# The last certain expert tile in two halves, and the two results of a token side by side: loaded in eight pieces, added by two engines, stored on two queues

## The chip, the cores and the metric

The kernel runs on one core of one Trainium2 chip. The time is device microseconds of that core for one execution. The kernel before took 618.88 us, the median of 6 runs (617.77 to 619.91). Lower is better. Engines are called as in the profile: PE (TensorE matmul) and PEld (its weight loads), DVE (VectorE), ACT (ScalarE), POOL (GpSimd) and SP (SyncE, which here only issues transfers).

## The reference, cut to what matters

The input is x of 4 batches with 512 tokens of 128 features, 2048 tokens in all. Attention comes first and its result is added to x. Then every token goes to two of eight experts, and the two weighted results are added to x:

```
combine = sum(one_hot(top2 experts) * weight)          # two experts per token
hact = up * gelu(gate)                                 # 512 hidden features per expert
out  = sum over the token's two experts of weight * (hact @ down_w[expert].T)
return x + out
```

## The kernel before, in words

**Attention** fills the first part of the execution. A planner (`route`, `plan`) works out, batch by batch, the two experts of each token and scatters each token's normalized row, with its weights and with the numbers of the rows where its two results belong, into an array `slots` in DRAM, so that tiles of 128 slots belong to one expert each. There are 39 possible tiles (`TILES`), of which 35 are certain (`sure`); the last four stand in nested `tc.If` blocks and run only where the counts call for them. In the profiled execution none of the four ran: the groups of L753, L754 and L766 have 35 instructions each.

**One expert tile t** has four steps. `load` (L683) issues three transfers on SP's queue: the rows, the gate and up weights, the down weights. `prepare` (L722) transposes the rows (PE L727, ACT L729) and takes each row's weight and target row (DVE L731, L736, L738). `up` (L742) does the 16 recorded matmuls of gate and up into one PSUM tile (PE L748), then Gelu over 128x512 (ACT L753) and the product of Gelu and up (DVE L754, 128x512, tile `act`). `down` (L756) does the 8 recorded matmuls with the down weights (PE L761), scales by the token's weight (DVE L766, tile `ye`), and scatters the 128 rows to the array `parts` in DRAM by an indirect transfer from POOL (L770), followed by a small POOL memset (L220).

**The order is written out by hand** (`tc.manual_schedule`). In the loop of L789 tile t's `up` comes first, then `prepare(t+1)`, then `down(t-1)`. So at the last certain tile, 34, DVE's queue holds: the product of tile 34, then the scaling of tile 33; after the loop `down(34)` follows. Then every engine passes the branches of the four spare tiles (L801). Where they are skipped, POOL runs one instruction (`INC_SWDGE_SEM`, at L801) that raises the semaphores which the skipped scatters would have raised.

**The end** (L808 to L817): a token's two results stand in `parts` at row p\*8 + k\*4 + c of their batch, for partition p, column c of 4 and choice k of 2. So the first results of a partition's four tokens lie together, and the second results behind them. SP waits for all scatters, then issues four loads of 512 KB, one per batch (L811). DVE adds, per batch, the first results and then the second results to x, 128x512 each (L814, eight instructions). ACT's queue stores each batch, 256 KB, when its two adds are done (L817). After that each engine comes to the end of the program (L863): a DRAIN, and a barrier in which POOL and SP wait for all.

```
for b in range(B):
    follow(nc.sync.dma_start(yy[:, b], both[b]), added)
for b in range(B):
    for k in range(TOP_K):
        nc.vector.tensor_tensor(xs[b], xs[b], yy[:, b, k * NT : (k + 1) * NT], ALU.add)
    nc.scalar.dma_start(out[b].rearrange("(p c) d -> p c d", p=P), xs[b])
```

Of the kernel before, what the change touches and what calls it, by code (L numbers as in the profile page):

```python
# [9 lines left out]
F32 = mybir.dt.float32  # L10
# [3 lines left out]
ALU = mybir.AluOpType  # L14
# [9 lines left out]
TOP_K = 2  # L24
# [7 lines left out]
def tile_attention_then_moe(  # L32
# [100 lines left out]
    def numbers(what, shape, pattern, base=0, channel=0):  # L133
        t = const.tile(shape, F32, tag=what, name=what)
        nc.gpsimd.iota(
            t, pattern, base=base, channel_multiplier=channel, allow_small_or_imprecise_dtypes=True
        )
        return t

    token = numbers("token", [P, B, NT], [[TOP_K * S, B], [1, NT]], base=-NONE, channel=TOP_K * NT)  # L140
    first = numbers("first", [P, E], [[N, E]])
    expert = numbers("expert", [P, E], [[1, E]])
    tile_no = numbers("tile_no", [P, TILES], [[1, TILES]])
# [78 lines left out]
    def follow(ins, scatters):  # L222

        for scatter in scatters:
            tc.add_manual_dep(
                ins.ins, scatter.ins.name,
                mybir.DependencyInfo(mybir.DependencyClass.Sync, mybir.DependencyReason.DATA),
                reason="reads what was scattered",
            )
# [267 lines left out]
    def route(g, hn, hT):  # L497
# [54 lines left out]
        for k in range(TOP_K):  # L552
# [2 lines left out]
        row = t8("row")  # L555
        nc.vector.tensor_tensor(row, top, wide(token[:, g, :]), ALU.mult)
        nc.vector.scalar_tensor_tensor(
            hn[:, :, D + E :], hits[:, 1], float(NT), row, ALU.mult, ALU.add
        )
        if late:  # L560
            yield from pause(1)
# [107 lines left out]
    def experts():  # L669


        NCH = WIDE // P
        GF = S // WIDE

        def value(at, most):
            return nc.values_load(
                at, engines=[mybir.EngineType.SP], min_val=0, max_val=most,
                skip_runtime_bounds_check_because="plan() bounds it: a tile is of an expert or spare",
            )

        got = {}

        def load(t):  # L683
            while t not in plans:
                assert others
                advance(others)
            new = {}
            if t >= sure:
                if not count:
                    count.append(nc.values_load(  # L690
                        needed[B - 1],
                        engines=[
                            mybir.EngineType.SP, mybir.EngineType.PE, mybir.EngineType.DVE,
                            mybir.EngineType.Activation, mybir.EngineType.Pool,
                        ],
                        min_val=0, max_val=TILES,
                        skip_runtime_bounds_check_because="plan() bounds it: it counts tiles",
                    ))
                new["cond"] = count[0] > t - STARTS[-2]
            mine, e_at, slot_at, scatters = plans[t]  # L700
            e = value(e_at, E - 1)
            at = value(slot_at, spare)
            gu = p4.tile([P, F2], F32, tag="gu", name=f"gu_{t}")
            dn = p4.tile([P, NF, D], F32, tag="down", name=f"down_{t}")
            xt = p4.tile([P, NCH, ROW], F32, tag="xt", name=f"xt_{t}")

            rows = nc.sync.dma_start(
                xt, slots[bass.ds(at, WIDE), :].rearrange("(c p) d -> p c d", p=P), **new
            )
            follow(rows, scatters)  # L710
            for scatter in filled[len(scatters) :]:
                tc.declare_no_dep(rows.ins, scatter.ins, reason="to slots that no tile has yet")
            read.append(rows)
            nc.sync.dma_start(
                gu, gu_t[:, bass.ds(e, 1), :].rearrange("p o f -> p (o f)"), **new
            )
            nc.sync.dma_start(
                dn, down_t[:, bass.ds(e, 1)].rearrange("p o f d -> p (o f) d"), **new
            )
            got[t] = xt, gu, dn  # L720

        def prepare(t):  # L722

            xt, gu, dn = got[t]
            tp = ps_tp.tile([P, NCH, P], F32, tag="tp", name=f"tp_e_{t}")
            for c in range(NCH):
                nc.tensor.transpose(tp[:, c, :], xt[:, c, 0:D], ident)  # L727
            xT = p2.tile([P, NCH * P], F32, tag="xeT", name=f"xeT_{t}")
            nc.scalar.copy(xT, tp.rearrange("p c t -> p (c t)"))  # L729
            of = small.tile([P, NCH, 2, E], F32, tag="of", name=f"of_{t}")  # L730
            nc.vector.tensor_tensor(  # L731
                of, xt[:, :, D:].rearrange("p c (i e) -> p c i e", i=2),
                plans[t][0].unsqueeze(1).to_broadcast([P, NCH, 2, E]), ALU.mult,
            )
            w = small.tile([P, NCH, 2], F32, tag="w", name=f"w_{t}")
            nc.vector.tensor_reduce(w, of, AX.X, ALU.add)  # L736
            row = small.tile([P, NCH], U32, tag="row", name=f"row_{t}")
            nc.vector.tensor_scalar_add(row, w[:, :, 1], float(NONE))  # L738
            act = p2.tile([P, NF, WIDE], F32, tag="act", name=f"act_{t}")
            got[t] = xT, gu, dn, w, row, act  # L740

        def up(t, f0):  # L742
            xT, gu, act = got[t][0], got[t][1], got[t][5]
            ps = ps_sc.tile([P, 2, GF, WIDE], F32, tag="sc", name=f"gu_{t}_{f0}")
            for g in range(GF):
                for j in range(2):
                    at = j * F + (f0 + g) * P
                    nc.tensor.matmul(  # L748
                        ps[:, j, g, :], gu[:, at : at + P], xT, start=True, stop=True
                    )  # L750
            yield
            ge = p3.tile([P, GF, WIDE], F32, tag="ge", name=f"ge_{t}_{f0}")
            nc.scalar.activation(ge, ps[:, 0], AF.Gelu)  # L753
            nc.vector.tensor_tensor(act[:, f0 : f0 + GF, :], ge, ps[:, 1], ALU.mult)  # L754

        def down(t):  # L756
            _, _, dn, w, row, act = got.pop(t)
            ps = ps_tp.tile([P, NCH, D], F32, tag="tp", name=f"dn_{t}")
            for c in range(NCH):
                for f in range(NF):  # L760
                    nc.tensor.matmul(  # L761
                        ps[:, c, :], act[:, f, c * P : (c + 1) * P], dn[:, f, :],
                        start=(f == 0), stop=(f == NF - 1),
                    )
            y = p3.tile([P, NCH, D], F32, tag="ye", name=f"ye_{t}")
            nc.vector.tensor_tensor(  # L766
                y, ps, w[:, :, 0:1].to_broadcast([P, NCH, D]), ALU.mult
            )
            for c in range(NCH):
                apart(added, nc.gpsimd.indirect_dma_start(  # L770
                    parts, bass.IndirectOffsetOnAxis(ap=row[:, c : c + 1], axis=0),
                    y[:, c, :], None, bounds_check=TOP_K * N - 1, oob_is_err=False,
                ))

        def ahead(t):

            for u in (t + 1, t + 2):
                if u < TILES and u not in loaded and (u in plans or u == t + 1):
                    load(u)
                    loaded.add(u)  # L780

        loaded, count = set(), []
        sure = TILES - SPARE_TILES
        ahead(-1)
        yield
        ahead(0)
        prepare(0)
        yield
        for t in range(sure):  # L789
            yield from up(t, 0)  # L790
            yield
            if t + 1 < sure:
                if t + 1 not in loaded:
                    ahead(t)
                prepare(t + 1)
            if t > 0:
                down(t - 1)
                ahead(t)
                yield
        down(sure - 1)  # L800
        with ExitStack() as inner:  # L801
            for t in range(sure, TILES):
                inner.enter_context(tc.If(count[0] > t - STARTS[-2]))
                prepare(t)
                yield from up(t, 0)
                ahead(t)
                down(t)
        both = parts.rearrange("(b p r) d -> b p r d", b=B, p=P)  # L808
        yy = p2.tile([P, B, TOP_K * NT, D], F32, tag="exT", name="yy")
        for b in range(B):  # L810
            follow(nc.sync.dma_start(yy[:, b], both[b]), added)  # L811
        for b in range(B):
            for k in range(TOP_K):
                nc.vector.tensor_tensor(  # L814
                    xs[b], xs[b], yy[:, b, k * NT : (k + 1) * NT], ALU.add
                )
            nc.scalar.dma_start(out[b].rearrange("(p c) d -> p c d", p=P), xs[b])  # L817

    hs, qkv, plans, needed, others = {}, {}, {}, {}, []
    filled, added = [], []  # L820
# [46 lines left out]
```

## Time and profile before

| what | value |
|---|---|
| median of 6 runs | 618.88 us (617.77 to 619.91) |
| the profiled execution's own time | 618.49 us |
| its span, first to last instruction | 616.78 us (1.71 us lie around it) |
| PE busy | 562.4 us (91% of the span) |
| DVE, ACT, POOL busy | 388.9, 352.0, 332.1 us |
| the last PE matmul ends | 599.84 us |
| loads of `parts` (L811) | 4, 512 KB each, first issued at 603.89 us |
| adds (L814) | 8, 690 ns each on average |
| stores (L817) | 4, 256 KB each, last issued at 613.43 us |

The page's PE row is at 9 or more tenths through nearly all of the span; the last slices, of 15.4 us each, fall to 8 and 0. Only those last 20 us hold instructions that the change touches. Times in what follows are microseconds from the start of the span. The granted TensorE clock was 0.977 on average.

### The profile page before, as it was taken

To read this page: it belongs to the slowest core of one execution; us is meant where nothing else is said; L and a number is where in the kernel's file an instruction comes from. 1 tells how busy PE (TensorE), PEld (TensorE's weight loads), DVE (VectorE), ACT (ScalarE), POOL (GpSimd) and SP (SyncE) were. 2 spreads that over 40 slices of the span, in tenths; PEclk is the share of its full clock that TensorE was granted. 3 is DMA by queue.
4 is the path that set the end of the run, shared out by engine and by line. 5 is a ranking of instruction groups with operands and counts; after the bars stand their busy time and mean duration, and the time that the engine had idled before them with its cause. 6 is when DMAs were issued, how large, how long until landed. Compare 5 with 4: busy or idle time off the path is not lost.

```text
span 616.8 us, 10390 instructions
## 1 busy us (share of the span) xinstructions
PE 562.4 (91%) x3363; PEld 344.8 (56%) x3363; DVE 388.9 (63%) x973; ACT 352.0 (57%) x896; POOL 332.1 (54%) x338
## 2 busy tenths in 40 slices
PE   3779999999999999999999999999989999499980
PEld 1235445446654544566454455654446898499980
DVE  1568666566677688666777875577893278144443
ACT  2467767776678766767776677677764122022220
POOL 3356554555557458755764686457575145433340
PEclk9899999999999999999999999999999999699995
DMA  8990000000000000200000005000002378589945
GB/s 237 300 236 1 2 0 2 1 0 2 2 1 0 1 2 20 69 8 2 0 1 0 12 25 173 2 2 1 1 16 82 104 257 253 192 258 311 321 163 205
DMA packets 38231, 50.32 MB, mean 82 GB/s; under 512 B 4115, under 2 KB 26517, under 8 KB 38176
## 3 DMA queue, kind: packets, MB, share of 16 engines
q1 hardware_dynamic: 34592, 43.50, 23.0%
q0 software_dynamic: 2144, 4.46, 2.0%
q10 hardware_dynamic: 1440, 1.67, 0.8%
q8 instruction: 28, 0.46, 0.3%
q14 instruction: 27, 0.22, 0.1%
HBM read 36.25 MB, written 15.29 MB: 84 GB/s over the span
## 4 chain that ended last, share of the span: by engine, by line
PE 69%; issue 8%; DVE 7%; POOL 6%; ACT 5%; DMA 5%; POOLq 0%; SPq 0%; DVEq 0%
PE sc L272 18%; PE av L315 18%; PE tp L305 16%; PE qp L254 5%; PE yp L339 5%; POOL parts L770 3%; DMA parts<-ye,row 3%; ACT ex L287 2%; PE gu L748 2%; DVE nmax L279 1%; ACT exT L415 1%; POOL slots L585 1%; ACT qT L256 1%; DMA yy<-parts 1%; DVE exT L417 1%
## 5 line engine op out<-in xcount | busy, mean ns | idle before, releaser
L296 POOL TENSOR_SCALAR ex<-ex,rden 128x512 f32<-128x512 f32 x128 | 221.1, 1729 | 168.1 <-DVE rden L295 166.3
L287 ACT ACTIVATE ex<-sc,nmax 128x512 f32<-128x512 f32 x256 | 176.1, 706 | 0.6 <-DVE nmax L279 0.6
L279 DVE TENSOR_REDUCE nmax<-sc 128x2 f32<-128x1024 f32 x128 | 150.5, 1217 | 8.0 <-PE sc L272 7.7
L305 PE MATMUL tp<-ident,ex 128*128 128x128 f32 x1024 | 131.3, 276 | 7.0 <-ACT exT L415 3.4
L272 PE MATMUL sc<-kT,qT 64*128 64x512 f32 x512 | 129.6, 623 | 8.2 <-ACT ex L287 7.5
L305 PEld LDWEIGHTS tp<-ident,ex 128*128 128x128 f32 x1024 | 112.9, 141 | 42.2 <-issue 24.6
L315 PE MATMUL av<-exT,v 128*64 128x512 f32 x512 | 128.4, 605 | 0.6 <-DVE exT L417 0.6
L415 ACT COPY exT<-tp 128x512 f32<-128x512 f32 x128 | 75.5, 590 | 49.0 <-PE tp L305 49.0
L272 PEld LDWEIGHTS sc<-kT,qT 64*128 64x128 f32 x512 | 43.9, 186 | 91.7 <-issue 52.0
L748 PE MATMUL gu<-xeT,gu 128*128 128x128 f32 x560 | 73.1, 285 | 10.9 <-ACT xeT L729 9.3
L770 POOL DMA_INDIRECT parts<-ye,row x35 | 34.4, 984 | 77.0 <-DVE ye L766 52.9
L295 DVE RECIPROCAL rden<-den 128x2 f32<-128x2 f32 x128 | 21.1, 165 | 86.5 <-ACT ex L287 82.7
L748 PEld LDWEIGHTS gu<-xeT,gu 128*128 128x128 f32 x560 | 67.0, 196 | 12.5 <-ACT xeT L729 9.7
L297 DVE TENSOR_SCALAR ex<-ex,rden 128x512 f32<-128x512 f32 x128 | 65.4, 511 | 4.5
L753 ACT ACTIVATE ge<-gu 128x512 f32<-128x512 f32 x35 | 20.9, 598 | 81.2 <-PE gu L748 63.3
L417 DVE COPY exT<-tp 128x512 f32<-128x512 f32 x64 | 44.0, 688 | 29.9 <-PE tp L305 29.8
L315 PEld LDWEIGHTS av<-exT,v 128*64 128x64 f32 x512 | 32.9, 136 | 51.1 <-issue 46.9
L754 DVE TENSOR_TENSOR act<-ge,gu 128x512 f32<-128x512 f32 x35 | 24.0, 686 | 58.2 <-ACT ge L753 31.5
L287 ACT ACTIVATION_READ_ACCUMULATOR ex<-sc,nmax 128x1 f32 x256 | 56.7, 221 | 0.0
L256 ACT ACTIVATE qT<-qp 128x512 f32<-128x512 f32 x32 | 19.1, 597 | 65.0 <-PE qp L254 65.0
L425 ACT COPY exT<-tp 128x512 f32<-128x512 f32 x64 | 39.6, 618 | 0.3 <-PE tp L305 0.3
L761 PE MATMUL dn<-down,act 128*128 128x128 f32 x280 | 38.3, 281 | 0.7 <-DVE act L754 0.5
(136 smaller groups left out, 435.3 us busy)
## 6 DMA issues: line engine op xcount, KB each, us to landing
gu<-in_gate_up_t_dram SPq DMA_DIRECT2D x37, 512.0 KB
down<-in_down_t_dram SPq DMA_DIRECT2D x37, 256.0 KB
slots<-blank SPq DMA_DIRECT2D x13, 720.0 KB
xt<-slots SPq DMA_DIRECT2D x37, 72.0 KB
yy<-parts SPq DMA_DIRECT2D x4, 512.0 KB
x<-in_x_dram SPq DMA_DIRECT2D x4, 256.0 KB
out_dram<-x ACTq DMA_DIRECT2D x4, 256.0 KB
parts<-ye,row POOLq DMA_INDIRECT x35
```

What stands on the lines that cost most here:

```text
L272: nc.tensor.matmul(sc[:, j, :], qT[p][half, t * P : (t + 1) * P], kT[half, :], start=True, stop=True)
L279: nc.vector.tensor_reduce(nmax, sc, AX.X, ALU.max, negate=True)
L287: nc.scalar.activation(ex[:, j, :], sc[:, j, :], AF.Exp, bias=nmax[:, j : j + 1], accum_out=den[:, j : j + 1],)
L296: nc.gpsimd.tensor_scalar_mul(ex[:, 0, :], ex[:, 0, :], rden[:, 0:1])
L297: nc.vector.tensor_scalar_mul(ex[:, 1, :], ex[:, 1, :], rden[:, 1:2])
L305: nc.tensor.transpose(tp[:, c, :], ex[:, j, c * P : (c + 1) * P], ident)
L315: nc.tensor.matmul(av[j * DH : (j + 1) * DH, :], v[:, c, :], exT[:, j, c, :], start=(c == 0), stop=(c == NT - 1),)
L415: nc.scalar.copy(*copies[0])
L417: nc.vector.tensor_copy(*copies[1])
L425: nc.scalar.copy(*copies[1])
L748: nc.tensor.matmul(ps[:, j, g, :], gu[:, at : at + P], xT, start=True, stop=True)
L770: apart(added, nc.gpsimd.indirect_dma_start(parts, bass.IndirectOffsetOnAxis(ap=row[:, c : c + 1], axis=0), y[:, c, :], None, bounds_check ...
```

## The change

Four things are changed together, all in the last 22 us; the program before them issues the same instructions in the same order.

1. **Halves.** The last certain tile's `up` is done as two halves of 256 columns: 8 recorded matmuls into one PSUM tile, 8 into another, two Gelus of 128x256 and two products of 128x256. `down` is split into `product` (matmuls) and `results` (scaling and scatter). On DVE the order is now: first half's product, scaling of tile 33, second half's product, scaling of tile 34.
2. **Rows side by side.** A token's two results go to rows p\*8 + c\*2 + k.
3. **Eight loads and split adds.** A piece is half the columns of a batch: 256 KB of results, 2 KB per partition in one run. SP issues eight loads. The adds are 128x256, two per piece: pieces 1, 3 and 5 on POOL, pieces 0, 2, 4, 6 and 7 on DVE.
4. **Eight stores** of 128 KB, 1 KB per partition: pieces 0, 2, 4, 6 on ACT's queue, pieces 1, 3, 5, 7 on SP's queue, behind the loads.

In the instruction order of the changed kernel each first add waits for the semaphore of its own load and each second add for the first. The eighth load uses the semaphore of the second load and waits until that one has landed. SP's store of piece 5 uses the semaphore of the store of piece 0 and waits for it too.

```diff
-    token = numbers("token", [P, B, NT], [[TOP_K * S, B], [1, NT]], base=-NONE, channel=TOP_K * NT)
+    token = numbers("token", [P, B, NT], [[TOP_K * S, B], [TOP_K, NT]], base=-NONE, channel=TOP_K * NT)
...
-            hn[:, :, D + E :], hits[:, 1], float(NT), row, ALU.mult, ALU.add
+            hn[:, :, D + E :], hits[:, 1], 1.0, row, ALU.mult, ALU.add
...
-        def up(t, f0):
+        def up(t, f0, n=GF):
...
-            ps = ps_sc.tile([P, 2, GF, WIDE], F32, tag="sc", name=f"gu_{t}_{f0}")
-            for g in range(GF):
+            ps = ps_sc.tile([P, 2, n, WIDE], F32, tag="sc", name=f"gu_{t}_{f0}")
+            for g in range(n):
...
-        for t in range(sure):
+        for t in range(sure - 1):
             yield from up(t, 0)
             yield
-            if t + 1 < sure:
-                if t + 1 not in loaded:
-                    ahead(t)
-                prepare(t + 1)
+            if t + 1 not in loaded:
+                ahead(t)
+            prepare(t + 1)
             if t > 0:
                 down(t - 1)
                 ahead(t)
                 yield
+
+        halves = [up(sure - 1, f0, GF // 2) for f0 in range(0, NF, GF // 2)]
+        for half in halves:
+            next(half)
+        rows = product(sure - 2)
+        for half in halves[:-1]:
+            next(half, None)
+        results(sure - 2, rows)
+        next(halves[-1], None)
+        ahead(sure - 1)
         down(sure - 1)
...
-        both = parts.rearrange("(b p r) d -> b p r d", b=B, p=P)
-        yy = p2.tile([P, B, TOP_K * NT, D], F32, tag="exT", name="yy")
-        for b in range(B):
-            follow(nc.sync.dma_start(yy[:, b], both[b]), added)
-        for b in range(B):
+
+        both = parts.rearrange("(b p c k) d -> b p c (k d)", b=B, p=P, k=TOP_K)
+        yy = p2.tile([P, B, NT, TOP_K, D], F32, tag="exT", name="yy")
+        half = NT // 2
+        pieces = [(b, slice(c, c + half)) for b in range(B) for c in range(0, NT, half)]
+        for b, c in pieces:
+            follow(
+                nc.sync.dma_start(yy[:, b, c].rearrange("p c k d -> p c (k d)"), both[b, :, c]),
+                added,
+            )
+        for i, (b, c) in enumerate(pieces):
+            by = nc.gpsimd if i in (1, 3, 5) else nc.vector
             for k in range(TOP_K):
-                nc.vector.tensor_tensor(
-                    xs[b], xs[b], yy[:, b, k * NT : (k + 1) * NT], ALU.add
-                )
-            nc.scalar.dma_start(out[b].rearrange("(p c) d -> p c d", p=P), xs[b])
+                by.tensor_tensor(xs[b][:, c], xs[b][:, c], yy[:, b, c, k], ALU.add)
+        for i, (b, c) in enumerate(pieces):
+            (nc.sync if i % 2 else nc.scalar).dma_start(
+                out[b].rearrange("(p c) d -> p c d", p=P)[:, c], xs[b][:, c]
+            )
```

More of the change, by code (lines that the diff above doesn't have):

```diff
@@ L751, in up, with product @@
             yield
-            ge = p3.tile([P, GF, WIDE], F32, tag="ge", name=f"ge_{t}_{f0}")
+            ge = p3.tile([P, n, WIDE], F32, tag="ge", name=f"ge_{t}_{f0}")
             nc.scalar.activation(ge, ps[:, 0], AF.Gelu)
-            nc.vector.tensor_tensor(act[:, f0 : f0 + GF, :], ge, ps[:, 1], ALU.mult)
-        def down(t):
-            _, _, dn, w, row, act = got.pop(t)
+            nc.vector.tensor_tensor(act[:, f0 : f0 + n, :], ge, ps[:, 1], ALU.mult)
+        def product(t):
+            dn, act = got[t][2], got[t][5]
             ps = ps_tp.tile([P, NCH, D], F32, tag="tp", name=f"dn_{t}")
@@ L764, in down, with results @@
                     )
+            return ps
+        def down(t):
+            results(t, product(t))
+        def results(t, ps):
+            _, _, _, w, row, _ = got.pop(t)
             y = p3.tile([P, NCH, D], F32, tag="ye", name=f"ye_{t}")
```

## The prediction

> **What bounds the kernel now.** I read the page's chain first, then the chain of waits from 585 us on, then the timeline of the last 20 us, then the lines L801 and L863. PE sets the pace up to about 600 us; the change touches only what follows. The chain there:
>
> ```profile
> 585.27 18.29 DMA parts<-ye,row
> 603.56 0.02 issue
> ...
> 603.89 0.34 SPq L811
> ...
> 604.75 5.87 DMA yy<-parts
> ...
> 610.65 0.70 DVE x L814
> ...
> 612.71 0.69 DVE x L814
> ```
>
> Columns are start, length, what. SP is released at 603.56, loads from 603.89, DVE starts the third batch at 610.65 when its load has landed, and the last add ends at 613.40. The last store is issued at 613.43; SP passes its wait for it at 615.46, and 1.32 us of waits and barrier end the span at 616.78. The 18.29 us belong to POOL's queue: its last scatter starts at 600.44 and ends at 601.41, and SP's release comes with the end of POOL's INC_SWDGE_SEM (602.09 to 603.62).
>
> How that last scatter came about, from the timeline (start, length, engine, line, operation):
>
> ```profile
> 597.30 0.60 ACT L753 ACTIVATE ge<-gu 128x512 f32<-128x512 f32 x1 [2.14 <-PE gu L748]
> ...
> 597.93 0.69 DVE L754 TENSOR_TENSOR act<-ge,gu 128x512 f32<-128x512 f32 x1 [1.53 <-ACTq L801]
> 598.54 0.28 DVE L766 TENSOR_TENSOR ye<-dn,w 128x128 f32<-128x128 f32 x1
> ...
> 598.68 1.16 PE L761 MATMUL dn<-down,act 128*128 128x128 f32 x8 [0.52 <-DVE act L754]
> ...
> 599.87 0.29 DVE L766 TENSOR_TENSOR ye<-dn,w 128x128 f32<-128x128 f32 x1 [1.05 <-PE dn L761]
> ```
>
> PE waits 0.52 us for the product of tile 34, then the chain Gelu, product, matmul, scaling runs with nothing beside it.
>
> **Halves: 0.25 us gained.** The 16 matmuls take 2.05 us from 595.22, so the first half ends at 596.24. A 256-wide Gelu lies between the 0.26 us of the 128-wide copy (L729) and the 0.60 of the 512-wide Gelu: 0.37. A 256-wide product lies between 0.28 (L766) and 0.69: 0.42. First product: 596.67 to 597.09. The scaling of tile 33 is now queued on DVE ahead of the second product and waits for that tile's matmuls, which end at 598.16: 598.19 to 598.47. The second product, whose Gelu is ready at 597.67, stands behind it: 598.50 to 598.92. PE does the first half of tile 34 after 598.16, the second from 598.98 for about 0.6. The scaling starts at 599.61 for 599.87, the scatter at 600.18 for 600.44. Bounds: 0 (both halves wait for the second product), and 0.55 (the second product not held by the scaling; matmuls follow at 598.16). I take 0.25, and all up to SP's release moves with it: first load at 603.64. The second PSUM buffer is free at 595.73, before it is wanted.
>
> **Rows side by side: 0.** Same scatters of 512-byte rows, same arithmetic with other constants. Its cover is that POOL's scatter row (0.97 us) doesn't depend on the target; if landing got slower, SP would wait for INC_SWDGE_SEM anyway until 603.3.
>
> **Loads: 0.1 us.** Eight issues of 0.34 to 0.43 us with 0.05 between put the last at 606.9; the eighth also waits for the second to land (about 606.9) and store issues wait behind it. Neither decides, since 2 MB keep the queues busy to 611. In the stretch 606 to 609 the transfers were 94.1% busy with 278 packets of 4 KB: 0.162 us each. In 612 to 617, 286 packets of 2 KB took 31.1%: 0.087 each. So 1024 packets of 2 KB on 16 engines are 5.6 us where 512 of 4 KB are 5.2: 0.35 later at the end of the loads, minus the 0.25 gained.
>
> **Adds.** DVE's 128x512 add is 0.69 us, its 128x8 add (L544) 0.17: a 128x256 add is 0.43, a piece 0.86. POOL's 128x512 add of two SBUF tensors took 1.27 us (L333, L449), its 128x4 one 0.20: 128x256 is 0.73; with 0.09 between dependent POOL instructions (L199 to L200) 0.82. The first batch, 512 KB, woke DVE at 607.47; pieces 0 and 1 are as many bytes, so with -0.25 and a quarter of 0.35 piece 1 wakes POOL at about 607.3. Six adds: the sixth starts at 607.3 + 5 x 0.82 = 611.4. Piece 5 is at three quarters of the loads: 610.65 - 0.25 + 0.26 (three quarters of 0.35) + 0.3 for the earlier stores that share the queues = 610.95, so the sixth starts no sooner than 610.95 + 0.82 = 611.8.
>
> Do POOL's and DVE's adds disturb each other? Two pairs of rows (POOL, then the DVE instruction beside it), start and length:
>
> ```profile
> 418.99 1.48 POOL L449 TENSOR_TENSOR x<-x,yn 128x512 f32<-128x512 f32 x1
> ```
>
> ```profile
> 418.86 0.49 DVE L297 TENSOR_SCALAR ex<-ex,rden 128x512 f32<-128x512 f32 x1
> ```
>
> ```profile
> 306.14 1.27 POOL L449 TENSOR_TENSOR x<-x,yn 128x512 f32<-128x512 f32 x1
> ```
>
> ```profile
> 306.91 0.79 DVE L297 TENSOR_SCALAR ex<-ex,rden 128x512 f32<-128x512 f32 x1
> ```
>
> Where DVE came first, POOL lost 0.20; where POOL came first, DVE lost 0.30. But small DVE products of two SBUF tensors (L553, 0.19 us) ran inside a POOL instruction of 1.78 us and lost almost nothing. So a DVE add costs POOL between 0 and a full turn of 0.43. Half of five meetings at 0.20 is 0.5: nearest to the large rows. The sixth POOL add then starts at **612.0** (611.0 at best: no loss, piece 1 at 607.0; 613.55 at worst: five full turns).
>
> The Trainium skill, page "SBUF — State Buffer", section "Who interferes with whom", speaks against the change: a VectorE instruction with two SBUF inputs and a GpSimd instruction that reads SBUF share a read interface, and whoever comes first holds it for the whole instruction. The L449 rows agree, the L553 rows don't; by the page the sixth add would start at 613.55, by the small rows at 611.8.
>
> **Stores.** 256 KB took 2.04 us from issue (613.43) to SP's wake (615.46). Half of the bytes are 0.3 less: 1.7. The eight stores together are 1024 packets of 1 KB; from 0.162 and 0.087 I put one at 0.05: 3.2 us for 2.8. SP's store of piece 7 stands behind that of piece 5, which waits for POOL (612.8): issued at 613.25, landed 614.95, 0.5 before the 615.46 of now.
>
> **What moves behind: POOL's end.** POOL had nothing to do after 603.6. Now its DRAIN comes after its adds. From the line L863, then L801:
>
> ```profile
> L863 POOLq DRAIN  x3: 40/107/5551, 603.6 to 616.5; - x3
> ...
> L863 DVEq DRAIN  x2: 19/374/728, 612.7 to 616.2; - x2
> ```
>
> ```profile
> L801 POOLq INC_SWDGE_SEM  x1: 1525/1525/1525, 602.1 to 602.1; - x1
> ```
>
> POOL's first DRAIN at the end took 5.55 us, 603.65 to 609.20, with no POOL operation open; today 6.8 us of cover remain until the barrier (615.98). The DRAIN ahead of any scatter (L856) took 0.18, the two after the barrier 0.11 and 0.04. So 5.55 belongs to what POOL had issued, 67 scatters, and not to the instruction as such. Bounds: 0.04, if the work runs out by itself by 609.2, and 5.55, if DRAIN does it when reached. I take 5.55: the same instruction with the same scatters before it is the nearest row. DVE's DRAIN started at 612.72, as the last add started (612.71); so POOL's starts with the sixth add: 612.0 + 5.55 = 617.55. The barrier took POOL's arrival 0.03 later, and from 615.98 to the end were 0.80: span 618.38, 1.60 more than 616.78. Against this execution's 618.49 that is 620.1; this execution is 0.39 below the median of 618.88, on which the forecast stands: **620.5 us**.
>
> **Cases.**
>
> A, forecast, 0.58: POOL's DRAIN ends last; 620.5. From the bounds of the sixth add (611.0 to 613.55): 619.5 to 622.0.
>
> B, 0.25, not slower: the 5.55 us run out beside the loads, and DRAIN is short. Then the last load decides. Now the loads' queue moves its last packets between 611.0 and 611.5; +0.1, and +0.65 for three stores amid the loads: DVE is woken at 612.2; two adds to 613.06; store to 614.8, against 615.46: 0.7 less, 618.2 us. With loads undisturbed 0.7 less again, 617.5. For it: short DRAINs elsewhere. Against it: by 603.65 the last scatter had long been issued, and still DRAIN took 5.55.
>
> C, 0.08: whatever fills 603.65 to 609.2 also keeps POOL from adding. Then six adds from 609.0 end at 613.9, piece 7's store is issued at 614.3 and lands at 616.0: 0.5 more, 619.4. For it: DVE's DRAIN lasts as long as its engine works. Against it: no POOL operation is recorded there.
>
> D, 0.09: no long DRAIN, but full turns between POOL and DVE: from 607.3 on 6 x 0.73 + 8 x 0.43 = 7.8, last add at 615.1, store landed at 616.9: 1.4 more, 620.3. It decides as soon as a DVE add is held for most of a POOL add.
>
> 0.2%, 1.24 us, is about what a measurement of this kernel can tell from no change: faster is under 617.64, slower over 620.12. Faster: 0.11 from B. Within: A 0.21, B 0.14, C 0.07, D 0.03 = 0.45. Slower: A 0.37, C 0.01, D 0.06 = 0.44. The range from B's better end to A's worst, 617.5 to 622.0, leaves out about 0.15; A's own is 619.5 to 622.0.
>
> **What would show it.** A: a POOL DRAIN of about 5.5 us that starts near 612, and the barrier after it. B: a DRAIN under 1 us, the end set by SP's wait for a store. C: POOL's first add starting near 609 though its load landed by 607. D: DVE adds over 0.7 us. Halves: the last scatter at 600.2. The forecast is wrong if DRAIN's length falls with the time since the last scatter, or if POOL's adds start much later than their loads land.

## The result, and the profile after

The changed kernel takes **622.87 us** (median of 19 runs, 620.9 to 624.38); the kernel before, in 40 runs of the same comparison, takes 619.1. The ratio is 1.0062 with a 95% interval of 1.005 to 1.0074: 3.8 us slower. The forecast was 620.5, its range ended at 622.0. The mechanism of case A is what the trace shows; two steps of its sum were wrong: when POOL's sixth add starts, and from when POOL's DRAIN counts.

The profiled execution after took 623.69 us, its span is 621.98. Against the profile before that is 5.2 us more, but not all of it belongs to the change. The second `qT` of ACT (L256), in a part of the program that is the same in both kernels, starts at 21.59 where it started at 19.36. Up to the first `qT` the profile after is even ahead (14.58 for 14.74); the 2.2 us come with the first eight matmuls of L272, 1.99 us before and 3.78 after, and the eight of L262 behind them, 1.10 and 1.70. The rows of L272, before and after (start, length, engine, line, operation):

```profile
15.39 1.99 PE L272 MATMUL sc<-kT,qT 64*128 64x512 f32 x8 [0.69 <-ACT qT L256]
```

```profile
15.23 3.78 PE L272 MATMUL sc<-kT,qT 64*128 64x512 f32 x8 [0.69 <-ACT qT L256]
```

So below I compare **tails**: from the first weight load of tile 34's gate and up matmuls (L748; 595.21 before, 597.30 after) to the end of the span. The tail was 21.57 us and is now 24.68: 3.11 more.

The timeline after, from the last two tiles to the last scatter (start, length, engine, line, operation):

```profile
598.21 0.28 DVE L774 TENSOR_TENSOR ye<-dn,w 128x128 f32<-128x128 f32 x1
598.50 0.38 ACT L753 ACTIVATE ge<-gu 128x256 f32<-128x256 f32 x1 [1.25 <-DVE ye L774]
...
598.92 0.42 DVE L754 TENSOR_TENSOR act<-ge,gu 128x256 f32<-128x256 f32 x1 [0.43 <-ACT ge L753]
...
600.29 0.29 DVE L774 TENSOR_TENSOR ye<-dn,w 128x128 f32<-128x128 f32 x1 [0.95 <-PE dn L761]
600.50 0.41 DVE L754 TENSOR_TENSOR act<-ge,gu 128x256 f32<-128x256 f32 x1
...
602.28 0.97 POOL L778 DMA_INDIRECT parts<-ye,row  x1 [0.38 <-DVEq L818]
```

The second product starts as the scaling of tile 33 ends, though its Gelu was ready at 599.77. The last scatter starts 4.98 after the mark; before it was 5.23 (600.44).

The timeline after, from the first adds on. A row gathers what follows one another without a stop, so its length is that of all x2, x4 or x6:

```profile
608.38 0.89 DVE L838 TENSOR_TENSOR x<-x,yy 128x256 f32<-128x256 f32 x2 [6.38 <-DMA yy<-parts]
609.26 1.52 POOL L838 TENSOR_TENSOR x<-x,yy 128x256 f32<-128x256 f32 x2 [5.93 <-DMA yy<-parts]
...
611.13 0.88 DVE L838 TENSOR_TENSOR x<-x,yy 128x256 f32<-128x256 f32 x2 [1.86 <-DMA yy<-parts]
...
612.20 3.35 POOL L838 TENSOR_TENSOR x<-x,yy 128x256 f32<-128x256 f32 x4 [1.42 <-DMA yy<-parts]
612.82 3.80 DVE L838 TENSOR_TENSOR x<-x,yy 128x256 f32<-128x256 f32 x6 [0.81 <-DMA yy<-parts]
```

POOL alone does two adds in 1.52 us, and DVE alone two in 0.88. Side by side from 612.82 on, it is slower: POOL's four take 3.35 us (0.72, 0.83, 0.90 and 0.78), and of DVE's six the second to the fourth take 0.83 each (613.28, 614.14 and 615.01), the others 0.42. POOL's last add runs from 614.77 to 615.55, DVE's last ends at 616.63.

Now the chain that ended last, for the same stretch (start, length, what):

```profile
587.19 18.21 DMA parts<-ye,row
605.40 0.02 issue
...
605.73 0.34 SPq L832
...
608.48 5.64 DMA yy<-parts
614.12 0.02 issue
614.14 0.84 DVE x L838
614.98 0.02 issue
615.01 1.18 DVE x L838 x2
616.18 0.02 issue
616.20 0.42 DVE x L838
```

This view ends with DVE's last add, 5.35 us before the end of the span, and shows no POOL behind it. Whoever stops here finds late loads and nothing else. The rest is in the line that ends the program, L888 (L863 before), and in SP's waits. Of the first view the columns are count, shortest/median/longest in ns, and first and last start; of the second, time waited, times, longest:

```profile
L888 POOLq DRAIN  x3: 40/113/6396, 614.7 to 621.7; - x3
L888 SPq DRAIN  x3: 7/7/7, 618.8 to 621.4; - x3
```

```profile
SPq L888 <- PEq L888: 3.0, 2, 2.4
...
SPq L888 <- DMA out_dram<-x: 1.0, 2, 0.7
```

POOL's first DRAIN at the end lasts from 614.73 to 621.13, and POOL's arrival at the barrier is recorded at 621.17. SP had its last store and stood at the barrier at 618.91. It then waited 2.26 us. The view puts that wait (2.4) down to PE's sequencer, but PE's DRAIN started at 601.9; the only arrival near 621.2 is POOL's. Before, SP's wait for the last store ended the span, and POOL's DRAIN (603.65 to 609.20) lay beside the loads.

### The profile page after: what moved, and what is told of

It is laid out like the page before. It is cut to its first block, busy times and chain, and to the rows that moved or that the text cites. A ratio compares the mean times of both kernels' runs of the same rounds, so it can differ in the third digit from the quotient of the medians.

```text
span 622.0 us, 10412 instructions
## 1 busy us (share of the span) xinstructions
PE 564.7 (91%) x3363; PEld 345.8 (56%) x3363; DVE 389.1 (63%) x976; ACT 352.1 (57%) x897; POOL 336.6 (54%) x344
## 4 chain that ended last, share of the span: by engine, by line
PE 70%; issue 8%; DVE 6%; POOL 6%; ACT 5%; DMA 4%; SPq 0%; POOLq 0%; DVEq 0%
PE sc L272 19%; PE av L315 18%; PE tp L305 16%; PE qp L254 5%; PE yp L339 5%; POOL parts L778 3%; DMA parts<-ye,row 3%; ACT ex L287 2%; PE gu L748 2%; ACT exT L415 1%; DVE nmax L279 1%; POOL slots L585 1%; ACT qT L256 1%; DMA yy<-parts 1%; PE kp L245 1%
## 5 line engine op out<-in xcount | busy, mean ns | idle before, releaser
L272 PE MATMUL sc<-kT,qT 64*128 64x512 f32 x512 | 131.5, 631 | 8.2 <-ACT ex L287 7.5
L272 PEld LDWEIGHTS sc<-kT,qT 64*128 64x128 f32 x512 | 44.6, 189 | 92.3 <-issue 52.8
L748 PE MATMUL gu<-xeT,gu 128*128 128x128 f32 x560 | 73.0, 285 | 10.8 <-ACT xeT L729 10.2
L748 PEld LDWEIGHTS gu<-xeT,gu 128*128 128x128 f32 x560 | 67.0, 196 | 12.5 <-ACT xeT L729 10.7
L297 DVE TENSOR_SCALAR ex<-ex,rden 128x512 f32<-128x512 f32 x128 | 65.4, 511 | 4.5
L753 ACT ACTIVATE ge<-gu 128x512 f32<-128x512 f32 (+1 forms) x36 | 21.1, 586 | 80.7 <-PE gu L748 61.6
L754 DVE TENSOR_TENSOR act<-ge,gu 128x512 f32<-128x512 f32 (+1 forms) x36 | 24.1, 670 | 54.8 <-ACT ge L753 28.3
L256 ACT ACTIVATE qT<-qp 128x512 f32<-128x512 f32 x32 | 19.1, 597 | 67.5 <-PE qp L254 67.5
```

The costliest lines, as they stand in the source:

```text
L272: nc.tensor.matmul(sc[:, j, :], qT[p][half, t * P : (t + 1) * P], kT[half, :], start=True, stop=True)
L297: nc.vector.tensor_scalar_mul(ex[:, 1, :], ex[:, 1, :], rden[:, 1:2])
L748: nc.tensor.matmul(ps[:, j, g, :], gu[:, at : at + P], xT, start=True, stop=True)
```

## The experiments

T is case A: POOL's DRAIN does work that belongs to the scatters, only once POOL's queue has come to it, and an operation of POOL after the loads pushes it to the end. Rivals: POOL's DRAIN is short and the loss is turns between POOL's and DVE's adds; the eight small loads; or the DRAIN is long because of POOL's adds themselves.

A table of tails is used throughout, one execution each: from the mark to the first load of `parts` (release), from there to the end of the last add, from there to the end of the span.

| kernel | release | loads and adds | rest | tail |
|---|---|---|---|---|
| before | 8.68 | 9.51 | 3.38 | 21.57 |
| `e2_pool_touch` | 8.68 | 8.92 | 5.13 | 22.73 |
| `e6_halves_only` | 8.43 | 9.11 | 3.38 | 20.92 |
| `e8_last_in_halves` | 8.43 | 9.40 | 3.15 | 20.98 |
| `e7_big_loads` | 8.43 | 10.01 | 2.88 | 21.31 |
| `e1_dve_adds` | 8.43 | 10.26 | 3.18 | 21.87 |
| `e3_pool_one` | 8.43 | 10.45 | 3.13 | 22.01 |
| `e5_early_drain` | 8.43 | 11.33 | 3.10 | 22.85 |
| after | 8.43 | 10.90 | 5.35 | 24.68 |

The first four have the same four loads; `e2_pool_touch` and `e6_halves_only` do the same DVE adds as before too. Yet their middle column runs from 8.92 to 9.51. So a difference of under 0.6 in that column between two executions says little. The release repeats to 0.01; the rest, where no DRAIN lies in it, is 3.38 with a last store of 256 KB and 2.88 to 3.18 with one of 128 KB.

**DVE does all adds.** The changed kernel without POOL's share:

```diff
-            by = nc.gpsimd if i in (1, 3, 5) else nc.vector
+            by = nc.vector
```

> The changed kernel with all sixteen adds of 128x256 on DVE, POOL adds nothing. Theory T (POOL's DRAIN costs 5.55 us from the end of POOL's last add, and that ends last): the DRAIN returns to its place behind INC_SWDGE_SEM, under the loads, and the DVE adds are 0.42 us again, not 0.83. Sixteen adds at 0.46 us spacing from the first load's wake are 7.4 us; the last add ends within 0.7 us of where it ends now, the span ends about 1.7 us after SP's last store wait. 2.5 to 3.3 us less than the changed kernel, 0 to 1 us more than the kernel before: 619.1 to 620.2 us. Rival L (the smaller loads and stores make the end late, DRAIN stands only beside them): no more than 0.5 us less than the changed kernel, 622.4 us or more.

Measured: 620.44 us against 619.75, ratio 1.0011 (0.999 to 1.0032). The 3.8 us are gone but for what can't be told from nothing. The lines of the end and of the adds:

```profile
L888 POOLq DRAIN  x3: 40/107/5551, 605.0 to 618.4; - x3
```

```profile
L838 DVE TENSOR_TENSOR x<-x,yy x16: 418/425/426, 607.8 to 615.1; 128x256 f32<-128x256 f32 x16
```

The DRAIN has the 5551 ns of the kernel before, lies at 605.0, and ends 5 us before the last add. Every DVE add takes 0.42 to 0.43 us once POOL adds nothing. That gives the loss to POOL's adds, not to the loads; DRAIN and turns went together here.

**One tiny operation of POOL, in the kernel before.** It copies one number of the last batch, so it waits for the last load; nothing else is changed:

```diff
             follow(nc.sync.dma_start(yy[:, b], both[b]), added)
+        nc.gpsimd.tensor_copy(gap, yy[0:1, B - 1, 0, 0:1])
```

> The kernel before, plus one POOL copy of a single element (1x1) of the last loaded batch: one tiny POOL instruction that waits for the fourth load; nothing else is changed, no adds on POOL, no smaller transfers. Theory T: POOL's DRAIN, 5.55 us, starts only after it, at about 612.1 in the clock of the profile of before, ends at 617.7, and the span ends 0.85 us later, 618.5 for 616.8: 1.5 to 2.0 us slower, about 620.8 us. Rivals (small transfers, or POOL and DVE in turns): no change, 619.1 us, DRAIN short or hidden.

Measured: 621.28 us against 619.75, ratio 1.003 (1.0014 to 1.0046). POOL's row in the timeline, then the line of the end:

```profile
611.85 0.19 POOL L812 COPY gap<-yy 1x1 f32<-1x1 f32 x1 [9.85 <-DMA yy<-parts]
```

```profile
L864 POOLq DRAIN  x3: 40/113/5779, 611.8 to 618.2; - x3
```

A copy of 0.19 us makes the kernel 1.9 us slower by the ratio, 1.5 between the medians. No add of POOL, no small load and no turn is in it: the move of the DRAIN is enough. The DRAIN is recorded from 611.84, as the copy starts, but it is longer by the copy: 617.62, its end, is 5.58 us after the copy's end (612.04). SP had its last store at 615.88, so 1.74 us of the tail are the DRAIN; they explain the whole column "rest" (5.13 for 3.38).

**POOL does one piece.** The changed kernel with `i == 1` for `i in (1, 3, 5)`.

> The changed kernel with only piece 1 on POOL, the other seven pieces on DVE. Theory T: POOL's second add ends about 1.6 us after its wake by the second load, DRAIN ends 5.55 us later, some 1.5 us before the barrier takes POOL: hidden. DVE has 14 adds. 2.8 to 3.8 us less than the changed kernel: 619.0 to 620.0 us. Rival L: 622.4 us or more. Rival turns (the doubled DVE adds are the loss): between the two, with DVE adds over 0.7 us beside POOL's.

Measured: 620.2 us against 619.75, ratio 1.0015 (0.9999 to 1.0031).

```profile
608.85 1.52 POOL L838 TENSOR_TENSOR x<-x,yy 128x256 f32<-128x256 f32 x2 [6.00 <-DMA yy<-parts]
```

```profile
L888 POOLq DRAIN  x3: 40/113/6336, 609.6 to 618.6; - x3
```

POOL's second and last add ends at 610.37, the DRAIN at 615.95: again 5.58 later. SP reaches the barrier at 617.99, so 2.05 us of cover are left and the DRAIN costs nothing. So POOL may work at the end of this kernel, with its 67 scatters, as long as it stops 5.6 us ahead of the others.

**A DRAIN ahead of POOL's adds.** The changed kernel with one more instruction. It puts POOL's adds off until the DRAIN is done:

```diff
+        nc.gpsimd.drain()
         for i, (b, c) in enumerate(pieces):
             by = nc.gpsimd if i in (1, 3, 5) else nc.vector
```

> The changed kernel with one more POOL DRAIN in front of its adds, behind INC_SWDGE_SEM. If DRAIN's time is work for the scatters issued before it and is done once: the first DRAIN takes 5.5 us (about 605.5 to 611.1 in the clock of the changed kernel's profile), POOL's adds start at 611.1 for 609.3, six of them end near 616.5, the last DRAIN takes under 0.5 us, the end is set by SP's waits for the stores: 1 to 2 us less than the changed kernel, 621 to 622 us. If DRAIN's time comes at the end of the program whatever went before: two DRAINs of 5.5 us, the adds later, 624 us or more. If it runs out with time: the early one 5.5, and no telling.

Measured: 620.4 us against 619.75, ratio 1.002 (1.0005 to 1.0034): 2.6 us of the 3.8 are back, more than the 1 to 2 that were expected. The added line, the line of the end, and the adds:

```profile
L835 POOLq DRAIN  x1: 5551/5551/5551, 603.2 to 603.2; - x1
```

```profile
L889 POOLq DRAIN  x3: 34/112/886, 612.9 to 617.6; - x3
```

```profile
L839 DVE TENSOR_TENSOR x<-x,yy x10: 412/558/939, 606.1 to 614.4; 128x256 f32<-128x256 f32 x10
L839 POOL TENSOR_TENSOR x<-x,yy x6: 716/782/898, 608.9 to 613.0; 128x256 f32<-128x256 f32 x6
```

The 5551 ns move to the place of the added instruction, and the DRAIN at the end, behind six adds, is 0.89 us: the last add (0.78) and 0.1. So the work is done once, belongs to what was issued before, and POOL's adds add nothing to it. The turns remain: DVE adds reach 0.94 us. The middle column, 11.33, also has POOL's late start in it (608.90, when the DRAIN ends).

**More scatters.** Into the kernel before go 33 scatters of 16 rows each, to an array that nobody reads:

```diff
+                if t < sure - 2:
+                    apart(more, nc.gpsimd.indirect_dma_start(
+                        extra, bass.IndirectOffsetOnAxis(ap=row[0:16, c : c + 1], axis=0),
+                        y[0:16, c, :], None, bounds_check=TOP_K * N - 1, oob_is_err=False,
+                    ))
```

> The kernel before, plus 33 scatters of 16 rows each, behind the result scatters of all tiles but the last two, into an array that nobody reads: 100 scatters for 67, 9104 scattered rows for 8576. If POOL's DRAIN takes its time per scatter (5.55 us / 67 = 83 ns each), it takes 8.3 us; if per scattered row, 5.9 us; if it is a fixed length, 5.55 us. DRAIN stands under the loads and stores (603.7 + 8.3 = 612.0, the barrier comes at 616), so the time doesn't change in any of the three, but for what the added scatters do to POOL's queue in the tiles (1 us each, POOL is idle for 1.7 us of 2.9 there): within 1 us.

Measured, in a single run: 646.58 us, so the time that was expected is missed by 28 us. The length of the DRAIN came as expected of a price per scatter:

```profile
L869 POOLq DRAIN  x3: 40/107/8246, 632.3 to 644.5; - x3
```

8.246 us for 100 scatters and 5.551 for 67 are 82.5 and 82.9 ns for each. A price by rows would have given 5.9, a fixed one 5.55. Each added scatter brings a small memset and a register move of POOL along; a price for each of these wouldn't stay the same (memsets 86 and 119, so 65 and 69 ns; moves 37 and 70, so 150 and 118). The 28 us lie in the expert tiles, not in the end. One part shows: DVE's instruction that writes the target rows (L739) now waits 9.4 us in eight waits for the added scatters; another is POOL's own 0.86 us for a scatter of 16 rows, hardly less than the 0.97 of one of 128. How the 28 us divide stays open.

**Halves alone.** The kernel before with part 1 of the change (`up` in halves, `product`, `results`) and nothing else.

> The kernel before with the halves alone: the last certain tile's gate and up in two halves, results, loads, adds and stores as before. Counted from the first gate and up matmul of tile 34 to the end of the span: 21.57 us in the kernel before. If the halves gain what the changed kernel's trace shows (the last scatter 0.24 us sooner): 21.3 us. If the gain is eaten by what comes behind (INC_SWDGE_SEM, loads): 21.6. The time can't tell this from no change: 619.0 to 619.7 us beside 619.7.

Measured: 618.65 us against 618.93, ratio 1.0003 (0.9987 to 1.0019). The release is 8.43 for 8.68, and so in every kernel with the halves: 0.25 us that a measurement of this kernel doesn't show. The rest of the 0.65 that its tail is shorter lies in the column that scatters.

**Four loads of 512 KB, all adds on DVE.** Against the changed kernel, with the pieces' adds and stores kept:

```diff
-        for b, c in pieces:
+        for b in range(B):
             follow(
-                nc.sync.dma_start(yy[:, b, c].rearrange("p c k d -> p c (k d)"), both[b, :, c]),
+                nc.sync.dma_start(yy[:, b].rearrange("p c k d -> p c (k d)"), both[b]),
                 added,
             )
...
-            by = nc.gpsimd if i in (1, 3, 5) else nc.vector
+            by = nc.vector
```

> The changed kernel with all adds on DVE (as in the first experiment), and with four loads of 512 KB for the eight of 256 KB; adds and stores stay in eight pieces. The first experiment ended 21.87 us after the first gate and up matmul of tile 34. If the pieces of 2 KB per partition make the loads late (7.8 us from first to last packet there, 6.5 in the kernel before): the last load lands about 1 us sooner, the adds are then bound by DVE (sixteen at 0.46 from the first 512 KB, 609.0 to 616.4 in that clock, 1 us later than its 615.5): 21.9 to 22.9 us, so no gain, DVE takes over. If DVE isn't the bound: 21.2 to 21.5 us.

Measured: 618.27 us against 618.93, ratio 0.9996 (0.9977 to 1.0016).

```profile
606.53 6.45 DVE L838 TENSOR_TENSOR x<-x,yy 128x256 f32<-128x256 f32 x16 [7.28 <-DMA yy<-parts]
```

DVE never stops: 16 narrow adds take 6.45 us where the eight wide ones, waits included, took 5.40 in the halves alone. So DVE does become what ends last, yet the tail is 21.31, less than was expected of that: the adds take 0.40 us each on average, since every second one is recorded as starting before the one ahead has ended, and the expectation had 0.46. The loads moved from 603.96 to 609.95, counted from the start of their first packet to the start of their last: 6.0 us, where eight loads took 7.8 (606.22 to 614.03 with DVE adding). That difference repeats: the five kernels here with four loads took 5.8 to 6.5 us, the four with eight loads 7.7 to 8.1. Of the 1.8 us only 0.25 arrive at the last add (10.26 for 10.01), because DVE is the slower one with large loads. That is within the scatter of the column.

**Only the last batch in halves.** Four loads, DVE adds of 128x512 for three batches and 128x256 for the fourth, whose halves are stored on two queues; halves and rows side by side kept:

```diff
+        for b in range(B):
+            for c in [slice(0, NT)] if b < B - 1 else [slice(0, half), slice(half, NT)]:
+                for k in range(TOP_K):
+                    nc.vector.tensor_tensor(xs[b][:, c], xs[b][:, c], yy[:, b, c, k], ALU.add)
+                (nc.sync if b == B - 1 and c.start == 0 else nc.scalar).dma_start(
+                    out[b].rearrange("(p c) d -> p c d", p=P)[:, c], xs[b][:, c]
+                )
```

> What the runs so far point to: halves as in the change, rows side by side, four loads of 512 KB, all adds on DVE, 128x512 for the first three batches and 128x256 twice for the last one; stores of 256 KB for the first three batches, and two of 128 KB on two queues for the last. 0.25 us from the halves and 0.3 us from a last store of half the size, minus 0.15 for two adds more: 21.1 to 21.3 us after the first gate and up matmul of tile 34, for 21.57 in the kernel before; 0.3 to 0.5 us less, which the time can hardly tell (ratio 0.999 to 1.000). Rival: the last store lands no sooner in halves, 21.4 us or more.

Measured: 619.06 us against 618.93, ratio 0.9999 (0.9982 to 1.0016). It was built from the parts that had gained something in a trace: 0.25 at the release, 0.23 at the last store. Half a microsecond is 0.08% and doesn't show. No kernel here is shown to be faster than the one before.

## Why the prediction was wrong in size, step by step

The sum for the tail, from the table: release -0.25; loads and adds +1.39; rest +1.97, which is 0.3 gained by the smaller last store (3.38 to 3.09, with the wait of 2.26 taken off) and 2.26 lost to the DRAIN. Together 3.11. Of the +1.39, 0.75 are there with DVE alone (`e1_dve_adds`), 0.64 come with the two engines; both rest on a column that scatters by 0.6.

- **Halves, 0.25 gained: right**, to 0.01 us, and for the reason given: the second product stood behind the scaling of tile 33.
- **Rows side by side, 0: not tried alone.** POOL's scatter row is 0.97 us as before, and the release shows nothing beside the halves' 0.25.
- **"POOL's starts with the sixth add", said of the DRAIN: wrong**, and the largest error. The step read a record of DVE's DRAIN that starts as the last add starts. POOL's DRAIN is recorded like that too, but its 5.58 us begin when the last operation ends, in three kernels alike (after, one copy, one piece). The sixth add is 0.78 us long, and 0.78 is what the sum lacked.
- **"The sixth POOL add then starts at 612.0": 0.68 too early.** That is 16.79 after the mark; it was 17.47. Piece 1 woke POOL at 609.26, 11.96 after the mark for a predicted 12.1, so the start was right. What failed is that the six adds were taken to follow one another from there, held up by piece 5 at most. Piece 3 came late, and no term had it: POOL stood still for 1.42 us until 612.20, and from then on its four adds followed without a stop. Pieces 0 to 3 are as many bytes as the first two batches before, whose load had landed 13.52 after the mark (608.73); piece 3's landed 14.83 after it (612.13). A load is recorded as sixteen landings: those of piece 3 came from 610.08 to 612.13, those of the second batch before from 608.22 to 608.73. I had the loads last 0.35 us more than the 6.5 they took (604.87 to 611.36, first packet's start to last packet's start); they took 1.3 more (7.8, 606.70 to 614.48). The price of a packet was nearly right, 84 ns in the median for 87, but the mean was 97. Why the landings of a small load lie so far apart stays open; stores ran between the loads only from 612.31 on. The best case of 611.0 also lay below the prediction's own floor of 611.8 from piece 5; with that floor case A's range would have begun at 620.3 for 619.5.
- **Turns, 0.5 for POOL: twice what was seen.** POOL's last four adds took 3.35 us, where 4 x 0.72 and three gaps of 0.08 are 3.1. DVE paid more: three adds of 0.83 for 0.42. I counted POOL's loss alone, since POOL was to end last. The pairs of rows that the estimate came from were no adds on DVE's side: L297 is a TENSOR_SCALAR, which reads one 128x512 tensor. The Trainium skill, page "SBUF — State Buffer", section "Who interferes with whom", has the later of a VectorE instruction with two SBUF inputs and a GpSimd instruction that reads SBUF wait for the whole of the other; for DVE the doubled adds agree in size, for POOL (0.06 to 0.18 longer) this case shows less than a full DVE add of 0.42.
- **Stores, 0.3 less: right**, 0.3 (3.38 to 3.09).
- **The barrier, 0.03 and 0.80: right** (0.04 and 0.81).

So the tail was forecast at 618.38 - 595.21 = 23.17 and came out at 24.68: 0.78 from the DRAIN's start, 0.68 from the sixth add, 0.05 from the rest. Onto the median another 0.7 came (3.8 us between the medians for 3.11 between the tails), which single executions don't settle, and 0.2 more lie in the kernel before, whose median was 619.1 in this comparison for the 618.88 of the forecast. Of the rivals, B (the 5.55 us run out by themselves) is refuted by `e2_pool_touch`: 10 us after the last scatter had ended (601.93) they were still to be paid in full. C is refuted by `e3_pool_one`: POOL's first add started at 608.85, within the 605.01 to 610.56 that the DRAIN fills in `e1_dve_adds`, whose mark is the same to 0.01 us. D's condition was met (DVE adds of 0.83) and SP came to the barrier 0.87 us later than before, counted from the mark; it decides only where the DRAIN doesn't lie behind it, as in `e5_early_drain`.

## What to carry to other kernels

Before an engine that had finished gets work at the end, look at its rows at the program's end line: what runs there under cover today is pushed behind the new work, and a very small operation is enough. Look there too when the chain of waits stops short of the span's end. Splitting loads and adds has a price per piece, here 16 narrow adds for 6.45 us against 5.4 for eight wide ones, and must gain more than that somewhere.

## What the runs showed of the hardware

- POOL's DRAIN after indirect scatters takes 83 ns for each scatter issued since the last DRAIN, whether of 128 or 16 rows (67: 5.551 us, 100: 8.246). With 67 it ends 5.58 us after POOL's last operation, even 10 us after the last scatter; a second DRAIN, with no scatter in between, ends 0.1 us after POOL's last operation.
- A scatter of 16 rows holds POOL for 0.86 us, one of 128 rows for 0.97.
- A store issued on ACT's queue while loads of SP's queue are in flight begins late: after, ACT issued its first store at 609.30, and its first packet moved at 612.31, 3.0 us later; before, with larger loads, 608.92 and 610.42, 1.5 us. With no load left, the last store before began 0.84 us after its issue (613.43 to 614.27).
- The first 20 us, whose matmuls are the same in both kernels, differ by 2.2 us between the two profiled executions: most of the first eight matmuls of L272 took 589 ns in one and 1057 in the other. Why stays open; a span is compared from a mark behind them.
